# Attention steps on one core: norm products and value transposes placed between the logits and the weighted sums, strips taken two at a time

## The chip, the core and the metric

The kernel runs on one core of a Trainium2 chip. The core has a matrix engine (TensorE, written PE in the profile, with its weight loads as PEld), a vector engine (VectorE, DVE), a scalar engine (ScalarE, ACT), a general engine (GpSimd, POOL) and a queue engine (SyncE, SP) that here only issues DMA transfers. Each engine works through its own instructions in the order in which they were issued to it and waits on semaphores for the others. Matrix products land in PSUM, everything else in SBUF or device memory.

The metric is the device time of one execution in microseconds, as a median of runs.

## What is computed

The input is one image of 48 channels, 256 x 256. Two residual layers are applied, each to a group-normalised copy of its input. The first is the one that matters here:

```python
qkv = einsum('bchw,oc->bohw', gn(x), w_qkv)      # 48 -> 144 channels
qkv = dwconv3x3(qkv, w_dw)
q, k, v = split(qkv, 3)
# 4x4 patches; 8 heads; per head 96 numbers for each patch
q, k = q / |q|, k / |k|                          # norm over the 96
attn = softmax(q^T k * temperature, axis=-1)     # per head, over all patches
out  = v attn                                    # 'bhcn,bhnm->bhcm'
out  = einsum('bchw,oc->bohw', fold(out), w_proj)
x    = x + out
```

There are 4096 inner patches; the padding adds a border of patches whose values are zero and which only enter the softmax's sum. The second layer multiplies windows of 64 x 64 pixels by three small matrices (over width, height and channels); nothing of it is touched.

## The kernel before

**Stages.** First the input's statistics, the 1x1 convolution for heads 0 and 1, and the depthwise convolution of head 0. Then the attention, eight heads one after the other. Then the projection with the first residual (L718 to L780), and the second layer (L783 to L915). The attention is by far the longest stage, and only it is changed.

**Steps of the attention.** For each head h a loop runs over g = 0 to 15 (L637). One step takes two blocks of 128 queries:

- `scores` (L553) makes the logits of one block: 24 products of 128 x 128 by 128 x 512 in four PSUM tiles named big (L334); ScalarE takes the exponential of each tile into `e` and its row sums into `zs` (L562). A step makes the second block of its own pair and then the first block of the next step's pair, 48 products in a row.
- `normalised` (L571) makes, on VectorE, four small instructions for each block that end in `vn`, the block's values over its softmax sums (L581).
- `weigh` (L584) is called for k = 0 to 3. Each call runs 32 products with 64 columns of `e` as the stationary operand and `vn` as the moving one (L591), alternately on the lower and upper half of the array's columns; within a call the first two products use the first block's `vn`, the third and fourth the second block's, and so on. VectorE adds each call's tile to `oacc` (L602). TensorE shows two records for each of these float32 products, so a call is 64 records.

The tiles named big, for logits, weighted sums and strips alike, share three PSUM buffers in rotation: a tile can be written when the tile three places earlier has been read.

**Work for the next head, done in the same steps.** Rows of the next head's depthwise convolution pass through the steps as a pipeline: in step g row g starts (`n.first`, ScalarE), row g-1 (`d`) gets its taps (L228, three after the first logits and five after the second), its square (L239), its sums `reduce` (L243, after the weighted sum k = 0), its norm product `norm` (L247, one product of 126 x 126 by 126 x 64 on TensorE, two records) and the inverse root `root` (L251 to L268, twelve small VectorE instructions) after k = 2, and `scale` (L273) after k = 3. Row g-2 (`p`) is split into a high and a low part (L282 on ScalarE, L286 on GpSimd) and stored. So norm and root of a row run in steps g = 1 to 10 of heads 0 to 6.

**Other work in the steps.** `turn` (L542) transposes a tile of values with four small TensorE products into a PSUM tile named pst (L545) and copies it with ScalarE: one call after k = 0 in steps 1 to 6 of head 0, and two calls (after k = 0 and k = 2) in steps 11 to 14 of heads 0 to 6. `store` (L604) transposes finished results with four products (L608): two calls after k = 0 of step 0 for the head before, and two after each of k = 1, 2 and 3 in step 15. The PSUM tiles of norms, turns and stores share two buffers (tag "one"). In head 0 each of the 64 places (h, g, k) also runs one `Strip` (L162): two products of 48 x 108 by 48 x 512 (L177, four records), a ScalarE copy (L180), and its loads and stores on SP's queue. Three input tiles `xs` and three output tiles `ot` are shared by the strips in rotation.

**Order.** The attention is inside `tc.manual_schedule()` (L631), so the order of the calls in the loop is the order of the instructions on each engine and on each DMA queue:

```python
                    for k in range(NK):
                        s = (h * NG + g) * NK + k
                        weigh(h, g, blocks, k)
                        if k == 0 and d:
                            d.reduce()
```

Of the kernel before, what the change touches and what calls it, by code (L numbers as in the profile page):

```python
# [8 lines left out]
F32 = mybir.dt.float32  # L9
# [20 lines left out]
CR = 9  # L30
# [15 lines left out]
def conv_preact_kernel(  # L46
# [62 lines left out]
    for z in range(3):  # L109
        for j in range(CH):  # L110
            p = (z * CH + j) * 6
# [46 lines left out]
    def both_halves(t, y, n, base=0):  # L158

        return [t[:, base + s * HALF + y : base + s * HALF + y + n, :] for s in range(2)]  # L160

    class Strip:  # L162
# [24 lines left out]
        def store(self):  # L187
            for s, rows in enumerate(both_halves(t1[1], 2 * self.j, 2, base=1)):
                nc.sync.dma_start(out=rows, in_=self.ot[:, 2 * s : 2 * s + 2, :])
# [140 lines left out]
    def logits(ps, qt, kts, q0, j):  # L330

        for i in range(2):
            for r in range(3):
                nc.tensor.matmul(  # L334
                    ps[:, i, :],
                    lhsT=qt[:, r, q0 : q0 + 128],
                    rhs=kts[2 * j + i][:, r // 2, :],
                    start=(r == 0),
                    stop=(r == 2),
                )  # L340
# [58 lines left out]
    with tc.tile_pool(name="xn", bufs=1) as xnp, tc.tile_pool(name="cst", bufs=1) as cst, tc.tile_pool(  # L399
        name="nps", bufs=2, space=PSUM  # L400
# [23 lines left out]
        for g, (w, k) in enumerate(((wq, P2), (wr, C))):  # L424
            m = w.shape[1]
# [60 lines left out]
    with tc.If(nc.values_load(large) > 0):  # L486
        with tc.tile_pool(name="sps", bufs=2, space=PSUM) as sps:
            for j in range(HALF // 2):
                w = Strip(j)
# [5 lines left out]
        with tc.tile_pool(name="mk", bufs=NM) as mk, tc.tile_pool(name="mq", bufs=2) as mq, tc.tile_pool(  # L495
            name="mps", bufs=2, space=PSUM
# [23 lines left out]
    with tc.tile_pool(name="ahead", bufs=2) as ah, tc.tile_pool(name="ae", bufs=3) as ae, tc.tile_pool(  # L520
        name="asm", bufs=6
# [6 lines left out]
        def load_key(h, m, eng=nc.sync):  # L528
            keys[h, m] = ah.tile([128, 2, 512], F32R, name="kt", bufs=14)
            load_keys(keys[h, m], h, m, eng)  # L530

        def load_query(h, g):
            queries[h, g] = ah.tile([128, 3, 256], F32R, name="qt", bufs=2)
            load_queries(queries[h, g], h, g)

        def load_value(h, m):

            vt = ah.tile([HD, 4 * 128], F32, name="vt")
            load(vt, qkv[h][2, 2], m * 512, (m + 1) * 512)
            values[h, m] = vt  # L540

        def turn(h, m):  # L542
            ps = one.tile([128, 4, HD], F32, name="pst", tag="one")
            for i in range(4):
                nc.tensor.transpose(ps[:, i, :], values[h, m][:, i * 128 : (i + 1) * 128], ident[:HD, :HD])  # L545
            vT = ah.tile([128, 4, HD], F32, name="vT", bufs=9)
            nc.scalar.copy(vT, ps)
            values[h, m] = vT
# [4 lines left out]
        def scores(h, nb):  # L553

            b = h * NB + nb
            e = ae.tile([128, NT], F32, name="e")
            zs = asm.tile([128, 4], F32, name="zs")
            kts = [keys[h, m] for m in range(NM)]
            for j in range(4):
                ps = big.tile([128, 2, 512], F32, name="big")  # L560
                logits(ps, queries[h, nb // 2], kts, nb % 2 * 128, j)
                nc.scalar.activation(  # L562
                    e[:, j * 1024 : (j + 1) * 1024],
                    ps.rearrange("p a b -> p (a b)"),
                    AF.Exp,
                    bias=nmx[:, b : b + 1],
                    accum_out=zs[:, j : j + 1],
                )
            return h, nb, e, zs

        def normalised(h, nb, e, zs):  # L571

            b = h * NB + nb
            zt = asm.tile([128, 1], F32, name="zt")
            nc.vector.tensor_reduce(zt, zs, AX.X, ALU.add)  # L575
            zu = asm.tile([128, 1], F32, name="zu")
            nc.vector.scalar_tensor_tensor(zu, e0[:, b : b + 1], float(NBORDER), zt, ALU.mult, ALU.add)  # L577
            rz = asm.tile([128, 1], F32, name="rz")
            nc.vector.reciprocal(rz, zu)
            vn = asm.tile([128, HD], F32, name="vn")  # L580
            nc.vector.tensor_scalar_mul(vn, values[h, nb // 4][:, nb % 4, :], rz)  # L581
            return e, vn
# [44 lines left out]
        strips = [[Strip(s)] if s < HALF // 2 else [] for s in range(NH * NG * NK + 2)]  # L627
# [3 lines left out]
        with tc.manual_schedule():  # L631
            load_query(0, 1)
            block = scores(0, 0)
            for h in range(NH):
                more = h + 1 < NH
                rows = {r: Depthwise(h + 1, r) for r in range(CR + 1)} if more else {}
                for g in range(NG):  # L637
                    p, d, n = rows.get(g - 2), rows.get(g - 1), rows.get(g)

                    if h == 0 and 0 < g <= 6:  # L640
                        load_value(0, g + 1)
                    if more and CR + 2 <= g < CR + 6:
                        for m in range(2):
                            load_value(h + 1, (g - CR - 2) * 2 + m)
                    if more and CR + 3 <= g < CR + 6:
                        for m in range(2):
                            load_key(h + 1, (g - CR - 3) * 2 + m)

                    blocks = [normalised(*block)]
                    block = scores(h, g * G + 1)  # L650
                    if more and g == NG - 1:
                        load_key(h + 1, 6)
                        load_key(h + 1, 7, nc.gpsimd)
                    if g + 2 < NG:
                        load_query(h, g + 2)
                    elif more:
                        load_query(h + 1, g + 2 - NG)
                    if p:
                        p.store((2,))
                    if d:  # L660
                        for t in range(1, 4):
                            d.tap(t)
                    second = block
                    if g + 1 < NG:
                        block = scores(h, (g + 1) * G)
                    elif more:
                        block = scores(h + 1, 0)
                    blocks.append(normalised(*second))
                    if d:
                        for t in range(4, 9):  # L670
                            d.tap(t)

                    if g == 0 and rows:
                        rows[0].load()
                    if p:
                        p.high()
                    if d:
                        d.square()
                    if n:
                        n.first()  # L680
# [5 lines that stand above are left out]
                        if k == 0 and p:  # L686
                            p.low(nc.gpsimd)
                            p.store((0, 1))
                        for w in strips[s]:
                            w.run(big.tile([128, 2, 512], F32, name="big"))  # L690
                        for w in strips[s + 2]:
                            w.load()
                        for w in strips[s - 1] if s else []:
                            w.store()
                        if k == 2 and d:
                            d.norm()
                            d.root()
                        if k == 2 and g + 1 in rows:
                            rows[g + 1].load()
                        if k == 3 and d:  # L700
                            d.scale()
                        if h == 0 and 0 < g <= 6 and k == 0:
                            turn(0, g + 1)
                        if more and CR + 2 <= g < CR + 6 and k in (0, 2):
                            turn(h + 1, (g - CR - 2) * 2 + k // 2)

                        if g == 0 and h > 0 and k == 0:
                            for m in range(6, 8):
                                store(h - 1, m)
                        if g == NG - 1 and k > 0:  # L710
                            for m in range(2 * k - 2, 2 * k):
                                store(h, m)
            for m in range(6, 8):
                store(NH - 1, m)
# [6 lines left out]
    with tc.tile_pool(name="pj", bufs=3) as pj, tc.tile_pool(name="pjs", bufs=1) as pjs, tc.tile_pool(  # L721
        name="pps", bufs=3, space=PSUM
# [60 lines left out]
    with tc.tile_pool(name="lx", bufs=3) as lx, tc.tile_pool(name="lz", bufs=2) as lz, tc.tile_pool(  # L783
        name="lr", bufs=2
    ) as lr, tc.tile_pool(name="ly", bufs=4) as ly, tc.tile_pool(name="ps1", bufs=2, space=PSUM) as ps1, tc.tile_pool(
        name="ps2", bufs=2, space=PSUM
# [170 lines left out]
```

## Time and profile before

| what | value |
|---|---|
| median of three runs | 3743.46 us (3741.68 to 3744.67) |
| the profiled execution's own time | 3747.01 us |
| its span | 3745.2 us |
| TensorE busy in the span | 3515.0 us (94%) |
| VectorE busy | 2186.7 us (58%) |
| ScalarE busy | 1717.9 us (46%) |
| GpSimd busy | 548.3 us (15%) |
| logits, L334 | 1438.6 us in 6144 records |
| weighted sums, L591 | 1419.5 us in 32768 records |

The attention's first full step starts at 320.76 us and the last weighted sums end near 3265 us. A start time in the timeline is microseconds from the span's start. Where one engine works without a pause, the difference between the starts of two neighbouring groups is what the first of them costs, and this is the number that is used below; the busy time of a TensorE group has a modelled end and overlaps its successor by some hundredths of a microsecond.

### The profile page before, as it was taken

To read this page: it belongs to the slowest core of one execution; us is meant where nothing else is said; L and a number is where in the kernel's file an instruction comes from. 1 tells how busy PE (TensorE), PEld (TensorE's weight loads), DVE (VectorE), ACT (ScalarE), POOL (GpSimd) and SP (SyncE) were. 2 spreads that over 40 slices of the span, in tenths; PEclk is the share of its full clock that TensorE was granted. 3 is DMA by queue.
4 is the path that set the end of the run, shared out by engine and by line. 5 is a ranking of instruction groups with operands and counts; after the bars stand their busy time and mean duration, and the time that the engine had idled before them with its cause. 6 is when DMAs were issued, how large, how long until landed. Compare 5 with 4: busy or idle time off the path is not lost.

```text
span 3745.2 us, 100375 instructions
## 1 busy us (share of the span) xinstructions
PE 3515.0 (94%) x44252; PEld 2913.5 (78%) x44252; DVE 2186.7 (58%) x3514; ACT 1717.9 (46%) x2667; POOL 548.3 (15%) x628
## 2 busy tenths in 40 slices
PE   2869999999999999999999999999999999855998
PEld 1337777788888888888888888888888888713776
DVE  5454774189529943994499349925982222266564
ACT  0225665555545545554555455545554444300333
POOL 2040121012111211221122112201220000000011
PEclk9989999999999999999999999999999999966999
DMA  7465665433323332333233323332333100299784
GB/s 163 145 145 148 178 171 166 146 90 97 79 81 86 89 82 78 88 89 85 75 94 85 82 74 95 85 80 84 94 77 84 36 19 20 60 236 190 122 141 91
DMA packets 274147, 386.49 MB, mean 103 GB/s; under 512 B 77010, under 2 KB 211522, under 8 KB 269480
## 3 DMA queue, kind: packets, MB, share of 16 engines
q1 hardware_dynamic: 234790, 264.95, 27.2%
q0 software_dynamic: 35424, 106.40, 12.3%
q10 hardware_dynamic: 3490, 8.64, 1.1%
q8 instruction: 351, 5.75, 0.6%
q14 instruction: 92, 0.75, 0.1%
HBM read 234.76 MB, written 144.90 MB: 101 GB/s over the span
## 4 chain that ended last, share of the span: by engine, by line
PE 87%; DMA 4%; issue 1%; DVE 1%; SPq 0%; ACT 0%; POOL 0%; POOLq 0%; ACTq 0%; DVEq 0%
PE big L334 38%; PE big L591 37%; PE pb L855 4%; PE pa L833 2%; PE pc L872 2%; PE big L177 2%; DMA pxt<-in_x_dram 1%; PE pst L545 1%; PE pt L608 1%; DMA x1s<-pxt 1%; PE pn L247 1%; DMA pot<-os__70 1%; DMA kt<-qkv 0%; DVE pxt L745 0%; DMA lxq<-x1s 0%
## 5 line engine op out<-in xcount | busy, mean ns | idle before, releaser
L562 ACT ACTIVATE e<-big,nmx 128x1024 f32<-128x1024 f32 x1024 | 1144.3, 1118 | 825.7 <-PE big L334 624.2
L334 PE MATMUL big<-kt,qt 128*128 128x512 f32 x6144 | 1438.6, 393 | 28.3 <-DMA qt<-qkv 20.1
L591 PEld LDWEIGHTS big<-vn,e 128*64 128x64 f32 x32768 | 1361.8, 137 | 81.4 <-ACT e L562 45.1
L591 PE MATMUL big<-vn,e 128*64 128x96 f32 x32768 | 1419.5, 247 | 2.9 <-DVE vn L581 1.9
L334 PEld LDWEIGHTS big<-kt,qt 128*128 128x128 f32 x6144 | 1146.4, 188 | 290.0 <-issue 40.5
L602 DVE TENSOR_TENSOR oacc<-big,oacc 128x768 f32<-128x768 f32 x480 | 458.2, 955 | 703.7 <-PE big L591 703.7
L228 DVE SCALAR_TENSOR_TENSOR acc<-pad,dwt,acc 126x1024 f32<-126x1024 f32 x592 | 766.8, 1295 | 35.9 <-ACT acc L209 19.7
L286 POOL TENSOR_TENSOR ol<-o,oh 126x1024 fp32r<-126x1024 f32 x78 | 187.0, 2398 | 964.6 <-DVE ss L243 834.8
L575 DVE TENSOR_REDUCE zt<-zs 128x1 f32<-128x4 f32 x256 | 38.7, 151 | 342.3 <-ACT e L562 342.3
L562 ACT ACTIVATION_READ_ACCUMULATOR e<-big,nmx 128x1 f32 x1024 | 195.9, 191 | 0.0
L840 DVE TENSOR_TENSOR lzt<-pa,cbias 128x864 f32<-128x864 f32 (+1 forms) x88 | 137.0, 1628 | 100.0 <-PE pa L833 100.0
L862 ACT COPY lyt<-pb 128x512 f32<-128x512 f32 x144 | 84.5, 586 | 216.0 <-PE pb L855 216.0
L612 POOL DMA_DIRECT2D os__70<-oo x128 | 65.2, 515 | 598.9 <-ACT oo L610 598.8
L855 PEld LDWEIGHTS pb<-wsb,lzt 128*64 128x64 f32 x2304 | 126.2, 138 | 30.1 <-issue 21.9
L239 ACT ACTIVATE sq<-acc 126x1024 f32<-126x1024 f32 x74 | 78.3, 1058 | 152.1 <-issue 111.6
L273 DVE TENSOR_TENSOR o<-acc,y 126x1024 f32<-126x1024 f32 x74 | 147.6, 1994 | 0.0
L855 PE MATMUL pb<-wsb,lzt 128*64 128x128 f32 x2304 | 142.4, 279 | 3.3 <-issue 3.3
L738 PE MATMUL pps<-pot,wp 96*96 96x512 f32 x128 | 77.7, 775 | 69.9 <-DMA pot<-os__70 69.9
L292 POOL DMA_DIRECT2D qkv<-o x72 | 56.3, 781 | 528.0 <-DVE zu L577 483.3
L180 ACT ACTIVATE ot<-big,bias 108x1024 f32<-108x1024 f32 x64 | 71.1, 1113 | 131.0 <-PE big L177 73.2
L738 PEld LDWEIGHTS pps<-pot,wp 96*96 96x96 f32 x128 | 26.6, 216 | 120.6 <-issue 117.5
L209 ACT ACTIVATE acc<-pad,dwt 126x1024 f32<-126x1024 f32 x74 | 84.1, 1137 | 78.1 <-DMA pad<-t 78.1
(122 smaller groups left out, 1877.3 us busy)
## 6 DMA issues: line engine op xcount, KB each, us to landing
pad<-t SPq DMA_DIRECT2D x238, 254.0 KB
t<-ot SPq DMA_DIRECT2D x128, 217.7 KB
qkv<-ol POOLq DMA_DIRECT2D x78, 336.0 KB, 6.2
qkv<-oh POOLq DMA_DIRECT2D x70, 336.0 KB, 5.6
qt<-qkv SPq DMA_DIRECT2D x176, 96.0 KB
xs<-in_x_dram SPq DMA_DIRECT2D x128, 96.0 KB
os__70<-oo POOLq DMA_DIRECT2D x128, 96.0 KB, 2.1
pxt<-in_x_dram SPq DMA_DIRECT2D x16, 768.0 KB
```

The source lines that it names most:

```text
L209: nc.scalar.mul(self.acc, self.pad[:, 0:KS, 0:W], dwt[:, self.h, 0:1])
L228: nc.vector.scalar_tensor_tensor(self.acc, self.pad[:, dy : dy + KS, dx : dx + W], dwt[:, self.h, tap : tap + 1], self.acc, ALU.mult, ALU.add,
L273: nc.vector.tensor_tensor(self.o.rearrange("p (a b) x -> p a b x", a=KS), self.acc.rearrange("p a (x b) -> p a b x", b=KS), self.y.rearran ...
L286: eng.tensor_sub(self.ol, self.o, self.oh.bitcast(F32))
L334: nc.tensor.matmul(ps[:, i, :], lhsT=qt[:, r, q0 : q0 + 128], rhs=kts[2 * j + i][:, r // 2, :], start=(r == 0), stop=(r == 2),)
L562: nc.scalar.activation(e[:, j * 1024 : (j + 1) * 1024], ps.rearrange("p a b -> p (a b)"), AF.Exp, bias=nmx[:, b : b + 1], accum_out=zs[:, ...
L591: nc.tensor.matmul(ps[p : p + 64, j // 4, j % 4 * HD : (j % 4 + 1) * HD], lhsT=e[:, mb * 128 + p : mb * 128 + p + 64], rhs=vn, start=(i == 0),
L602: nc.vector.tensor_add(oaccs[h, k], ps[:, :, : 4 * HD], oaccs[h, k])
L738: nc.tensor.matmul(ps[:, i : i + 2, :], lhsT=wp, rhs=ot[:, ki * KS + i : ki * KS + i + 2, :], start=True, stop=True,)
L840: nc.vector.tensor_tensor(zv[:, :, y0 : y0 + n, :], pa[:, :, : n * T3 * C].rearrange("p s (y k) -> p s y k", y=n), cbias.rearrange("p (u v ...
L855: nc.tensor.matmul(pb[s * WS : (s + 1) * WS, i, :], lhsT=zts[u][:, t * C + c + i, :], rhs=wsb[:, t, :], start=True, stop=True,)
L862: nc.scalar.copy(yt[:, t, :], pb.rearrange("p i x -> p (i x)"))
```

## The change

Five calls change their places; no instruction is added, and none is removed.

- `norm` and `root` of a row move from after k = 2 of step g to the beginning of step g+1, in front of the logits, where the row is called `p`; `scale` moves from after k = 3 to the middle of the next step's logits.
- All `turn` calls of a step, and the two `store` calls of step 0, move in front of the first weighted sum, behind the logits.
- Strips run in pairs after k = 1 and k = 3. Their loads follow in pairs at the same places, and their stores follow in pairs at k = 2 and at k = 0 of the next step.

```diff
                     blocks = [normalised(*block)]
+                    if p:
+                        p.norm()
+                        p.root()
                     block = scores(h, g * G + 1)
...
                     if p:
+                        p.scale()
                         p.store((2,))
...
                     if g == 0 and rows:
                         rows[0].load()
+
+                    if h == 0 and 0 < g <= 6:
+                        turn(0, g + 1)
+                    if more and CR + 2 <= g < CR + 6:
+                        for m in range(2):
+                            turn(h + 1, (g - CR - 2) * 2 + m)
+                    if g == 0 and h > 0:
+                        for m in range(6, 8):
+                            store(h - 1, m)
                     if p:
                         p.high()
...
                             p.low(nc.gpsimd)
                             p.store((0, 1))
-                        for w in strips[s]:
-                            w.run(big.tile([128, 2, 512], F32, name="big"))
-                        for w in strips[s + 2]:
-                            w.load()
-                        for w in strips[s - 1] if s else []:
-                            w.store()
-                        if k == 2 and d:
-                            d.norm()
-                            d.root()
+                        if s % 2:
+                            for w in strips[s - 1] + strips[s]:
+                                w.run(big.tile([128, 2, 512], F32, name="big"))
+                            for w in strips[s + 1] + strips[s + 2]:
+                                w.load()
+                        elif s:
+                            for w in strips[s - 2] + strips[s - 1]:
+                                w.store()
                         if k == 2 and g + 1 in rows:
                             rows[g + 1].load()
-                        if k == 3 and d:
-                            d.scale()
-                        if h == 0 and 0 < g <= 6 and k == 0:
-                            turn(0, g + 1)
-                        if more and CR + 2 <= g < CR + 6 and k in (0, 2):
-                            turn(h + 1, (g - CR - 2) * 2 + k // 2)
-
-                        if g == 0 and h > 0 and k == 0:
-                            for m in range(6, 8):
-                                store(h - 1, m)
+
```

## The prediction

> **What bounds the kernel.** I read the page's busy times first, then the timeline of TensorE in single steps, then VectorE's timeline in the same steps. The page:
>
> ```profile
> PE 3515.0 (94%) x44252; PEld 2913.5 (78%) x44252; DVE 2186.7 (58%) x3514; ACT 1717.9 (46%) x2667; POOL 548.3 (15%) x628
> PE   2869999999999999999999999999999999855998
> PEclk9989999999999999999999999999999999966999
> ```
>
> In the fourth to the thirty-fourth slice TensorE is at nine tenths or more, from 320 us on without a pause, and its granted clock is 1.00 in every stretch of 200 us from 400 to 3000. So here the time of a step is the sum of what stands in TensorE's order, and whatever shortens that order shortens the kernel, as long as nobody makes TensorE wait. A step of head 4 with a norm product, and one of head 7, which has nothing between:
>
> ```profile
> 2264.02 8.14 PE L591 MATMUL big<-vn,e 128*64 128x96 f32 x192
> 2272.09 0.43 PE L247 MATMUL pn<-ss,same 126*126 126x64 f32 x2
> 2272.45 2.86 PE L591 MATMUL big<-vn,e 128*64 128x96 f32 x64
> 2275.24 11.17 PE L334 MATMUL big<-kt,qt 128*128 128x512 f32 x48
> ```
>
> ```profile
> 3110.00 11.17 PE L334 MATMUL big<-kt,qt 128*128 128x512 f32 x48
> 3121.10 10.78 PE L591 MATMUL big<-vn,e 128*64 128x96 f32 x256
> ```
>
> By start differences (the next logits start at 3131.81), 256 records of weighted sums cost 10.71 us, 192 cost 8.07, 64 cost 2.79: 2.64 for each 64, and **0.15 for each time the run is left**. The norm product costs 0.36 before a weighted sum. The whole step costs 22.33 against 21.81, so one tiny product costs 0.52.
>
> **What a small product costs elsewhere.** Transposes stand before weighted sums at 0.48 for four (472.12 to 472.60), but between logits:
>
> ```profile
> 291.56 0.49 PE L545 MATMUL pst<-ident,vt 96*128 96x96 f32 x4
> 291.83 1.18 PE L334 MATMUL big<-kt,qt 128*128 128x512 f32 x4
> 292.85 0.49 PE L545 MATMUL pst<-ident,vt 96*128 96x96 f32 x4
> 293.13 7.10 PE L334 MATMUL big<-kt,qt 128*128 128x512 f32 x30
> ```
>
> 0.28 (292.85 to 293.13): returning to weighted sums costs 0.20 that returning to logits does not. The result transposes (L608) say the same, 1.01 against 0.84. A norm product before logits isn't in the trace; 0.36 less 0.17 to 0.20 gives 0.16 to 0.19, and its bounds are 0.16 and the full 0.36. I take 0.18. Going from logits to transposes: logits records come every 0.227 us (11.17 for 48 less 5.73 for 24, over 24), so 48 take 10.88 and the change to weighted sums 0.22 of the 11.10. In the rows above four records take 1.02, that is 0.91 and 0.11. So I take 10.99 for logits before transposes, bounds 10.88 and 11.10, by that row.
>
> **TensorE, heads 1 to 6.** Steps as they are and as they become:
> - g=0 (two result transposes move ahead): 22.98 becomes 11.10+1.01+10.71 = 22.82, **-0.16** (also in head 7).
> - g=1 (its norm goes to g=2): 22.33 becomes 21.81, **-0.52**.
> - g=2 to 10: 0.18+11.10+10.71 = 21.99 instead of 22.33, **-0.34**, if nothing waits.
> - g=11 (a norm arrives, two turns join): 0.18+10.99+0.28+0.48+10.71 = 22.64 instead of 23.08, **-0.44**.
> - g=12 to 14: 10.99+0.28+0.48+10.71 = 22.46 instead of 23.10, **-0.64**.
> - g=15 is unchanged.
>
> **VectorE is the new risk.** The root and scale now stand between the step's start and the second block's vn, which the third product of the first weighted sum needs. Its order in a step, from before:
>
> ```profile
> 2254.67 2.00 DVE L273 TENSOR_TENSOR o<-acc,y 126x1024 f32<-126x1024 f32 x1
> 2256.57 0.16 DVE L575 TENSOR_REDUCE zt<-zs 128x1 f32<-128x4 f32 x1
> ...
> 2257.35 3.93 DVE L228 SCALAR_TENSOR_TENSOR acc<-pad,dwt,acc 126x1024 f32<-126x1024 f32 x3
> 2261.19 0.15 DVE L575 TENSOR_REDUCE zt<-zs 128x1 f32<-128x4 f32 x1
> ...
> 2261.77 0.27 DVE L581 TENSOR_SCALAR vn<-vT,rz 128x96 f32<-128x96 f32 x1
> 2261.95 6.57 DVE L228 SCALAR_TENSOR_TENSOR acc<-pad,dwt,acc 126x1024 f32<-126x1024 f32 x5
> 2268.44 0.95 DVE L602 TENSOR_TENSOR oacc<-big,oacc 128x768 f32<-128x768 f32 x1
> 2269.69 1.22 DVE L243 TENSOR_REDUCE ss<-sq 126x64 f32<-126x1024 f32 x1 [0.31 <-ACT sq L239]
> ```
>
> Today vn is ready at 2262.04, 2 us before the weighted sum at 2264.02. After the change, counted from the norm product's start: the last addition starts at 0.12 (as after every run of weighted sums) and takes 0.87, the first block's four instructions 0.78, the root 3.05 (2250.75 to 2253.80), the scale 1.90, three taps 3.84, the second block's four until vn 0.58, vn 0.27: 11.41. TensorE sees it 0.05 later:
>
> ```profile
> 3246.54 0.39 PE L591 MATMUL big<-vn,e 128*64 128x96 f32 x4
> 3248.79 5.34 PE L591 MATMUL big<-vn,e 128*64 128x96 f32 x124 [1.87 <-DVE vn L581]
> ```
>
> Here vn started at 3248.47 and ended at 3248.74; four records, two products, had run, and nothing but the wait is lost. So vn counts from 11.46; TensorE reaches its fifth record at 0.18+11.10+0.165 = 11.45. They meet: a wait of 0.01, period 22.00, -0.33. Further on: five taps until 17.81, the first addition, the reduce at 19.06 (ScalarE's square, as now, 1.25 after the taps), the second addition until 21.07. The fourth weighted sum needs the first addition's buffer at 19.4 and has it by 18.8. VectorE is free at 22.0, and its next addition is due at 22.12: it fits with 0.1 to spare. That thin margin is the main risk. A norm that costs 0.36 would not add to a wait; it replaces it.
>
> Sum for a head: 0.16+0.52+9x0.33+0.44+3x0.64 = 6.0; six heads **-36.1**, head 7 -0.16.
>
> **Head 0, with strips.** A pair costs 2x1.045; two runs of 128 records 5.43 each (1014.35 to 1019.78); together 15.04 instead of 4x(2.79+1.045) = 15.34. But three buffers go round: the third weighted sum takes that of the second, which the second addition frees, and that stands behind the reduce. VectorE, now starting with the root at 0.47: 3.05+1.90+3.84+0.76+6.48 makes 16.50, reduce at 17.71, second addition from 18.85, free at 19.87. TensorE wants it at 0.18+11.10+5.43+2.09 = 18.80, or 19.16 with a turn. So a new wait of 1.08 or 0.71, and a step of 27.39 either way. g=2 to 6: 27.28 becomes 27.39, +0.55 in all; g=7 to 10: from 26.80, +2.36; g=1: 27.30 to 26.51; g=11: 27.39 to 26.97; g=12 to 14: 27.42 to 26.79; g=15 loses one interruption, 0.16; g=0 waits for ScalarE's first row either way. Sum **-0.4**. On SP's queue the stores of a pair come one call later, behind the query loads, and the loads of a pair's second input wait for the pair's first product; each still lands some 8 us ahead of its use. The value loads, issued 0 to 5 us into the step, now are needed at 11.2 instead of 15 us; 168 KB landed in 3.5 us elsewhere.
>
> **Sum.** -36.7 on the profiled execution's 3747.0 gives 3710.3. Its own time lies 3.5 above the median of the runs, so the median becomes 3706.8, **3707 us**.
>
> **A rule that speaks against it.** GpSimd's subtraction (2.36 us) runs from the reduce's end, at 20.3, until 0.6 of the next step; in before it never ran beside a VectorE instruction with two inputs in SBUF, and after the change it still ends before the root. The Trainium skill, "SBUF — State Buffer", section "SBUF: two separate sides", says that such an instruction and a GpSimd one exclude each other for the whole instruction. By it the sum stands as long as they don't meet, and a VectorE chain 1.6 us later would lose up to the subtraction's rest; no run here shows that. On the other side "TensorEngine Tiling (Array Packing)", "Key Properties", says that changing the tiling mode drains TensorE; logits and transposes have one mode, and by it the 0.11 above would be gone too, some 3 us more gained.
>
> **Rivals.**
> - *The interruptions cost the same in the new place*: 0.36 for a norm, 0.48 for every turn, 11.10 for logits. Then g=2 to 10 gain 0.16 each, g=12 to 14 0.33, g=11 loses 0.05: 3.9 a head, 23.5 for six, head 0 loses some 2: 3722 us. The 0.28 and 0.84 speak against it. 13%.
> - *Head 0's waits are longer* (a pair's copies, stores or the value loads come late): 1 to 3 us in each of 16 steps, 16 to 48 us: 3723 to 3755 us. For it: TensorE did wait 2.6 us for a strip's copy at 315.88. Against: the leads above. 10%.
> - *vn comes later than worked out*, by 0.3 us in 54 steps: 16 us, 3723 us. 10%.
> - *Slower: VectorE's chain becomes the bound.* Place: root and scale ahead of the second vn. Every 0.1 us costs 5.4; from 0.7 us the gain is gone, from 0.82 the kernel is slower by 0.2%. The price is bounded by a whole subtraction falling into the chain, 54x2.36 = 127 us, 3834 us. The margins above speak against it. 5%.
> - The forecast, 3697 to 3718 us: 62%. Its lower end is head 0 without its waits (8 us) and a strip pair 0.1 cheaper (3 us).
>
> Some 0.2% (7.5 us) is what a measurement can tell from no change. The range, **3697 to 3736**, takes in the forecast, the first and third rivals and part of the second. Faster (below 3736): 62+13+10+4 = 89, with a little taken off for what I overlooked 87%; within 0.2%: 6%; slower: 7%.
>
> **What will show it.** Right: steps g=2 to 10 of heads 1 to 6 at 22.0, the norm product before logits at 0.18, g=12 to 14 at 22.46, VectorE almost without a pause in g=2 to 10; head 0 at 27.39 for g=2 to 10 with a wait for an addition (L602) before the third weighted sum. Wrong: TensorE waiting for vn (L581) by more than 0.1 at the first weighted sum, strips waiting for `ot` or `xs`, transposes waiting for `vt`.

## The result and the profile after

The changed kernel takes 3737.34 us (median of 20 runs, 3731.5 to 3748.8), the kernel before 3741.89 in 20 runs beside it: a ratio of 0.999 [0.9982, 0.9999]. The change gains some 4.5 us where 37 were forecast; by the interval it is between 0.4 and 6.7. The profiled execution took 3738.23 us, its span is 3736.4.

The page of the changed kernel, with its line of the chain that ended last (shares of the span by engine):

```profile
PE 3478.8 (93%) x44252; PEld 2909.0 (78%) x44252; DVE 2218.8 (59%) x3514; ACT 1706.6 (46%) x2667; POOL 544.7 (15%) x628
...
PE   2869999999999999999999999999999999955998
...
PEclk9989999999999999999999999999999999966999
...
PE 65%; DVE 16%; issue 5%; DMA 4%; ACT 1%; SPq 1%; POOL 0%; DVEq 0%; ACTq 0%; POOLq 0%
```

The same line of the chain in the kernel before:

```profile
PE 87%; DMA 4%; issue 1%; DVE 1%; SPq 0%; ACT 0%; POOL 0%; POOLq 0%; ACTq 0%; DVEq 0%
```

TensorE is busy for 36 us less than before, and the span shrinks by only 9. So TensorE's own work became shorter, and it now waits. That 36 lies so close to the forecast gain is partly chance: the forecast had new waits of head 0 in its sum, and the busy time counts a part of each wait as work. The chain says for whom TensorE waits: VectorE has 16% of it, and had 1% before. The slices can't show this, since a wait of 0.4 us in 22 leaves a nine a nine. VectorE executes the same 3514 instructions and is busy for 32 us longer: some of them must have become slower. Among the groups, one moved by far more than the rest: L260, the integer step that starts the inverse root, takes 576 ns on average instead of 195, and with 70 executions that alone is 26.6 of the 32 us.

TensorE's timeline in head 4 (start, duration, then the wait in front of it and who ended it):

```profile
2270.13 0.43 PE L247 MATMUL pn<-ss,same 126*126 126x64 f32 x2
2270.37 11.16 PE L334 MATMUL big<-kt,qt 128*128 128x512 f32 x48
2281.46 0.39 PE L591 MATMUL big<-vn,e 128*64 128x96 f32 x4
2282.26 10.62 PE L591 MATMUL big<-vn,e 128*64 128x96 f32 x252 [0.41 <-DVE vn L581]
2292.80 0.43 PE L247 MATMUL pn<-ss,same 126*126 126x64 f32 x2
```

The norm product before the logits costs 0.24 (2270.13 to 2270.37). The logits take 11.09, four records run, and then TensorE stands until 2282.26: 0.80 from 2281.46, of which four records explain 0.165. The rest, 0.63, is the wait; the profile shows 0.41 of it as idle. From norm to norm the step is 22.67 us, not 22.00, and more than the 22.33 of before. VectorE in the same step:

```profile
2271.89 0.22 DVE L251 TENSOR_SCALAR n<-pn 126x64 f32<-126x64 f32 x1
2272.14 0.69 DVE L260 TENSOR_SCALAR y<-n 126x64 int32<-126x64 int32 x1
...
2275.20 0.31 DVE L268 TENSOR_SCALAR y<-y,nmul,nadd 126x64 f32<-126x64 f32 x1
2275.60 2.00 DVE L273 TENSOR_TENSOR o<-acc,y 126x1024 f32<-126x1024 f32 x1
2277.53 3.91 DVE L228 SCALAR_TENSOR_TENSOR acc<-pad,dwt,acc 126x1024 f32<-126x1024 f32 x3
...
2281.93 0.27 DVE L581 TENSOR_SCALAR vn<-vT,rz 128x96 f32<-128x96 f32 x1
```

vn ends at 2282.20, 12.07 after the norm product's start, and the fifth record starts at 12.13. The working had 11.46. The 0.67 lies in two places. L260 takes 0.69 instead of 0.20, that is 0.50; and the scale L273 starts 0.40 after L268's start, where the last addition, which stood there before, started 0.22 after it, that is 0.18. What GpSimd did meanwhile in the changed kernel:

```profile
2268.49 2.37 POOL L286 TENSOR_TENSOR ol<-o,oh 126x1024 fp32r<-126x1024 f32 x1 [12.52 <-DVE ss L243]
2270.81 0.98 POOL L292 DMA_DIRECT2D qkv<-oh  x1
2271.75 1.06 POOL L292 DMA_DIRECT2D qkv<-ol  x1
```

The subtraction L286 ends at 2270.86, well ahead of the root, as the prediction said. But behind it GpSimd issues the transfers of the two parts, each for about 1 us, and L260 stands from 0.39 us into the second one until its very end (2272.81 against 2272.83). In the kernel before the same instructions lay like this, first GpSimd, then VectorE:

```profile
2250.99 1.00 POOL L292 DMA_DIRECT2D qkv<-oh  x1
2252.00 1.00 POOL L292 DMA_DIRECT2D qkv<-ol  x1
```

```profile
2251.00 0.20 DVE L260 TENSOR_SCALAR y<-n 126x64 int32<-126x64 int32 x1
```

There L260 began within 0.04 us of the beginning of an issue, in all 54 steps, and ran through in 0.20. Behind it come nine instructions (L265 to L267) that ran through the issues in 0.22 to 0.23, and L268 begins at 2253.58, when both issues are over. In the changed kernel it begins 0.29 to 0.41 into the second issue in all 54 and takes 0.68 to 0.72. The trace of before never had it in that place.

One row inside the changed kernel supports the reading. In g=2 of heads 1 to 6 there is a norm, but no parts to be sent yet; L260 takes 0.20 there, and the step takes 22.19.

All steps, from logits to logits (a step holds the norm product of the next one). Each number is the usual one of its row; single steps differ, such as g=0 of head 1, which takes 23.15 in the changed kernel:

| steps | before | after | kernel "best" below |
|---|---|---|---|
| heads 1 to 6: g=0 | 22.98 | 22.69 | 22.70 |
| g=1 | 22.33 | 22.08 | 22.08 |
| g=2 | 22.33 | 22.19 | 22.03 |
| g=3 to 10 | 22.33 | 22.67 | 22.03 |
| g=11 | 23.08 | 22.47 | 22.46 |
| g=12 to 14 | 23.10 | 22.51 | 22.51 |
| g=15 | 24.99 | 25.01 | 25.01 |
| head 0: g=2 to 10 | 27.28, from g=7 26.80 | 27.38 | 26.33, from g=7 26.08 |

The attention, from the logits of g=1 in head 0 to those of g=1 in head 7, went from 2614.7 to 2612.3 us: -2.4. The rest of the profiled difference lies ahead of and behind the attention, where no instruction was changed, and is how two executions differ.

In head 0 a pair of strips stands behind 128 records. TensorE in the changed kernel:

```profile
447.41 5.50 PE L591 MATMUL big<-vn,e 128*64 128x96 f32 x128 [0.99 <-DVE oacc L602]
452.84 1.97 PE L177 MATMUL big<-xs,wr 48*108 48x512 f32 x8
454.74 0.43 PE L247 MATMUL pn<-ss,same 126*126 126x64 f32 x2
```

That is the foretold wait for the second addition, in the foretold place. By start differences it is 1.03 to 1.06 in g=2 to 6, where a transpose stands ahead of it, and 1.37 to 1.41 in g=7 to 10; 0.71 and 1.08 were forecast.

### The profile page after: what moved, and what is told of

The parts are those of the page before. It is cut to its first block, busy times and chain, and to the rows that moved or that the text cites. A ratio compares the mean times of both kernels' runs of the same rounds, so it can differ in the third digit from the quotient of the medians.

```text
span 3736.4 us, 100361 instructions
## 1 busy us (share of the span) xinstructions
PE 3478.8 (93%) x44252; PEld 2909.0 (78%) x44252; DVE 2218.8 (59%) x3514; ACT 1706.6 (46%) x2667; POOL 544.7 (15%) x628
## 4 chain that ended last, share of the span: by engine, by line
PE 65%; DVE 16%; issue 5%; DMA 4%; ACT 1%; SPq 1%; POOL 0%; DVEq 0%; ACTq 0%; POOLq 0%
PE big L591 35%; PE big L334 21%; DVE acc L228 7%; PE pb L858 4%; PE pa L836 2%; PE pc L875 2%; DVE oacc L602 1%; DMA x1s<-pxt 1%; PE big L177 1%; DMA pxt<-in_x_dram 1%; DVE y L267 1%; DVE z L265 1%; DVE z L266 1%; DVE y L260 1%; DVE vn L581 1%
## 5 line engine op out<-in xcount | busy, mean ns | idle before, releaser
L591 PE MATMUL big<-vn,e 128*64 128x96 f32 x32768 | 1400.5, 247 | 32.4 <-DVE vn L581 21.3
L602 DVE TENSOR_TENSOR oacc<-big,oacc 128x768 f32<-128x768 f32 x480 | 453.5, 954 | 677.3 <-PE big L591 671.1
L286 POOL TENSOR_TENSOR ol<-o,oh 126x1024 fp32r<-126x1024 f32 x78 | 187.4, 2403 | 897.4 <-DVE ss L243 786.4
L273 DVE TENSOR_TENSOR o<-acc,y 126x1024 f32<-126x1024 f32 x74 | 148.4, 2005 | 6.3
```

What stands on the lines that cost most here:

```text
L273: nc.vector.tensor_tensor(self.o.rearrange("p (a b) x -> p a b x", a=KS), self.acc.rearrange("p a (x b) -> p a b x", b=KS), self.y.rearran ...
L286: eng.tensor_sub(self.ol, self.o, self.oh.bitcast(F32))
L591: nc.tensor.matmul(ps[p : p + 64, j // 4, j % 4 * HD : (j % 4 + 1) * HD], lhsT=e[:, mb * 128 + p : mb * 128 + p + 64], rhs=vn, start=(i == 0),
L602: nc.vector.tensor_add(oaccs[h, k], ps[:, :, : 4 * HD], oaccs[h, k])
```

## Experiments

Two theories stood against each other. **A**: L260 is held up by the transfer issues of GpSimd, and with the late scale it delays the second vn; the rest of the change is worth what was forecast. **B**: VectorE's chain in its new order is too long by itself, whatever GpSimd does. The ratios are to the kernel before, on the same chip.

### One part alone

The norm product, the root and the scale moved, nothing else ("norm_only", against before):

```diff
                     blocks = [normalised(*block)]
+                    if p:
+                        p.norm()
+                        p.root()
...
                     if p:
+                        p.scale()
...
-                        if k == 2 and d:
-                            d.norm()
-                            d.root()
...
-                        if k == 3 and d:
-                            d.scale()
```

> Only the norm product, root and scale are moved as in the change; turns, stores and strips stay as in before. Theory A (VectorE's chain to the second vn is 0.67 us longer than I worked out: 0.5 because the root's second instruction, L260, stands still while GpSimd issues the transfer of the low part, 0.18 because the scale now follows the root's last instruction directly): in heads 1 to 6 the steps g=3 to 10 take 22.67 us against 22.33, g=2 some 22.2, so this part alone loses about 2.3 us a head, ratio to before about 1.003 (some 3753 us). Rival B (the chain is not the cause, the gain was lost elsewhere): the steps take 22.0 and the ratio is about 0.995.

Measured: 3760.73 us, ratio 1.005 [1.0038, 1.0063]. This part alone is a loss, larger than expected. Its steps g=3 to 10 take 22.67, as in the whole change. VectorE in g=2, where GpSimd issues nothing, and in g=3; then GpSimd in g=3:

```profile
2250.16 0.20 DVE L260 TENSOR_SCALAR y<-n 126x64 int32<-126x64 int32 x1
...
2272.35 0.72 DVE L260 TENSOR_SCALAR y<-n 126x64 int32<-126x64 int32 x1
```

```profile
2272.04 1.01 POOL L292 DMA_DIRECT2D qkv<-ol  x1
```

2272.35 is 0.31 into the issue, and 2273.07 is its end within 0.02. In head 0 this kernel also waits for a strip's copy, which the expectation had not counted, and most steps there take 27.86 instead of 27.28; TensorE there:

```profile
454.57 2.86 PE L591 MATMUL big<-vn,e 128*64 128x96 f32 x64 [0.64 <-ACT ot L180]
```

The transposes moved alone ("turns_only", against before):

```diff
+                    if h == 0 and 0 < g <= 6:
+                        turn(0, g + 1)
+                    if more and CR + 2 <= g < CR + 6:
+                        for m in range(2):
+                            turn(h + 1, (g - CR - 2) * 2 + m)
+                    if g == 0 and h > 0:
+                        for m in range(6, 8):
+                            store(h - 1, m)
...
-                        if h == 0 and 0 < g <= 6 and k == 0:
-                            turn(0, g + 1)
-                        if more and CR + 2 <= g < CR + 6 and k in (0, 2):
-                            turn(h + 1, (g - CR - 2) * 2 + k // 2)
-                        if g == 0 and h > 0 and k == 0:
-                            for m in range(6, 8):
-                                store(h - 1, m)
```

> Only the turns of all steps and the two stores of step 0 are moved in front of the first weighted sum. Theory A: nothing waits, the steps g=11 to 14 of heads 1 to 6 take 22.5 instead of 23.1, some 2.4 us a head, with the stores and head 0 some 18 us in all, ratio about 0.995. Rival B (moved turns give nothing once other things are equal): ratio 1.000.

Measured: 3727.37 us, 0.996 [0.9945, 0.9974]. The steps g=11 to 14 take 22.48 to 22.53, as forecast. Some is given back in head 0, where the value loads now come late (TensorE's timeline):

```profile
474.99 0.55 PE L545 MATMUL pst<-ident,vt 96*128 96x96 f32 x4 [1.31 <-DMA vt<-qkv]
```

With the strips in pairs, in the whole change, the same transposes don't wait.

The strips in pairs alone ("strips_only", against before):

```diff
-                        for w in strips[s]:
-                            w.run(big.tile([128, 2, 512], F32, name="big"))
-                        for w in strips[s + 2]:
-                            w.load()
-                        for w in strips[s - 1] if s else []:
-                            w.store()
+                        if s % 2:
+                            for w in strips[s - 1] + strips[s]:
+                                w.run(big.tile([128, 2, 512], F32, name="big"))
+                            for w in strips[s + 1] + strips[s + 2]:
+                                w.load()
+                        elif s:
+                            for w in strips[s - 2] + strips[s - 1]:
+                                w.store()
```

> Only the strips are paired. Theory A: a pair costs 1.90 instead of 2.09 us, and without the moved root the second addition is in time, so there is no wait for L602 before the third weighted sum: head 0 gains some 8 us, ratio about 0.998. Rival B (the wait in head 0 comes from pairing alone): the third weighted sum waits some 1 us in each of nine steps and the gain is near 0.

Measured: 3742.01 us, 1.0009 [0.9997, 1.0021]: no gain that the interval tells from none, where A had expected a small one. Most steps of head 0 take 26.3 to 27.0 us, so the pairs do save there, and no step waits for the second addition: that wait, which B had foretold, takes the moved root as well. But the profiled execution loses it again in one place. TensorE, and then two stretches of the same execution (length, then for each engine its busy time and instructions, PEclk, DMA share, GB/s):

```profile
434.16 3.87 PE L177 MATMUL big<-xs,wr 48*108 48x512 f32 x8 [5.19 <-DMA xs<-in_x_dram]
437.96 12.85 PE L334 MATMUL big<-kt,qt 128*128 128x512 f32 x48
```

```profile
434.00:438.00 4.00, 3.84 (x9) 1.53 (x9) 3.50 (x3) 1.11 (x1) 0.00 (x0) 0.50 0.89 203
442.00:446.00 4.00, 4.00 (x19) 3.31 (x18) 0.00 (x0) 3.13 (x7) 0.00 (x0) 1.00 0.52 163
```

A strip's input came late, TensorE stood for 5.19 us, and then the granted clock was 0.50: eight records took 3.87 instead of 1.97, and the logits 12.85 instead of 11.17. With 5.19, 1.90 and 1.68 the wait costs 8.8 us in all. On SP's queue the four loads of the pair were issued from 425.00 to 432.08, behind twelve query loads (414.20 to 421.38) and four stores (421.48 to 424.96). Whether every execution of this kernel has the wait, one profile can't say.

### The transfer issues taken away from GpSimd

The whole change, with the two stores of heads 1 to 6 on SP's queue ("after_sp", against after):

```diff
                             p.low(nc.gpsimd)
-                            p.store((0, 1))
+                            p.store((0, 1), nc.sync if h else nc.gpsimd)
```

> The whole change, and in heads 1 to 6 the stores of the high and low parts are issued from SP's queue instead of GpSimd's. Theory A: L260 takes 0.20 instead of 0.70 us, the second vn comes 0.5 earlier, steps g=3 to 10 take 22.2 instead of 22.67, some 23 us gained on the changed kernel, ratio to before about 0.993. Rival B (L260 is slow for another reason, or the chain is long all the same): L260 stays at 0.7 or the steps stay at 22.67, ratio 0.999.

Measured: 3711.42 us, 0.992 [0.9902, 0.9937]. TensorE, and L260, in the same step of head 4:

```profile
2258.14 0.43 PE L247 MATMUL pn<-ss,same 126*126 126x64 f32 x2
2258.38 11.15 PE L334 MATMUL big<-kt,qt 128*128 128x512 f32 x48
2269.46 10.96 PE L591 MATMUL big<-vn,e 128*64 128x96 f32 x256
2280.34 0.43 PE L247 MATMUL pn<-ss,same 126*126 126x64 f32 x2
```

```profile
2260.14 0.20 DVE L260 TENSOR_SCALAR y<-n 126x64 int32<-126x64 int32 x1
```

L260 takes 0.20 again, and the step 22.20 instead of 22.67. VectorE's order is the same as in the changed kernel, so B falls as the main cause. Weighted sums of 10.88 (2269.46 to 2280.34) instead of 10.71 show what remains, the 0.17 by which vn still comes late.

### The chain shortened, and the reduce moved

One tap fewer between the scale and the second vn ("after_taps"), and this together with the stores on SP ("after_sp_taps"); against after:

```diff
-                        for t in range(1, 4):
+                        for t in range(1, 3):
...
-                        for t in range(4, 9):
+                        for t in range(3, 9):
```

> The changed kernel with two taps instead of three ahead of the second vn (six behind it). The vn is then ready some 1.3 us earlier and TensorE has nothing to wait for there. Theory A (the block on L260 makes VectorE's whole round longer than TensorE's): VectorE has only 0.19 us of pause in a round of 22.67, so the steps g=3 to 10 come down to 22.48 only, some 9 us gained on the changed kernel, ratio to before about 0.9965. Rival B (only the place of the vn in VectorE's order counts): the steps come down to TensorE's own 22.04, some 30 us, ratio about 0.991.

> The changed kernel with both: the high and low parts of heads 1 to 6 stored from SP's queue, and two taps ahead of the second vn. Theory A: L260 at 0.20 and the vn in time, VectorE's round is 21.98 and TensorE's 22.04, so the steps g=2 to 10 take 22.05 against 22.19 with the queue alone, some 8 us less than that, ratio about 0.990. Rival B: no further gain once the queue is moved, ratio 0.992.

Measured: 3705.38 us, 0.9903 [0.9887, 0.9919], and 3704.37 us, 0.9901 [0.9883, 0.992]; both have steps of 22.03. That the taps add something to the moved queue is seen in the steps (22.20 in after_sp); the intervals of the times overlap. For after_taps that is B's number and not A's. But the profile shows why the run doesn't decide between them: GpSimd and VectorE of after_taps,

```profile
2255.63 1.06 POOL L292 DMA_DIRECT2D qkv<-ol  x1
```

```profile
2255.87 0.20 DVE L260 TENSOR_SCALAR y<-n 126x64 int32<-126x64 int32 x1
```

L260 now begins 0.24 into the issue (0.13 to 0.26 in all 54 steps), and runs through. A shift of some 0.15 us had taken it out of the place where it is held. The edit had removed the suspected cause as well as the length.

The reduce after k = 1 instead of k = 0, so that the second addition no longer stands behind it ("after_reduce", against after), and all three together ("after_all"):

```diff
-                        if k == 0 and d:
+                        if k == 1 and d:
                             d.reduce()
```

> The changed kernel with the reduce behind the second addition instead of the first. Theory A: in head 0 the third weighted sum no longer waits for the second addition, nine steps come down from 27.38 to 26.4 or below, some 9 us; in heads 1 to 6 GpSimd's work starts 0.9 us later, the issue of the high part instead of the low part now falls on L260, which stays slow, and the steps stay near 22.6: ratio about 0.9965. Rival B (L260 is slow only beside the second of the two issues): it falls to 0.2 and the steps to some 22.2, ratio about 0.990.

> The changed kernel with all three: stores of heads 1 to 6 from SP's queue, two taps ahead of the second vn, the reduce behind the second addition. Theory A: steps g=2 to 10 of heads 1 to 6 at 22.04, head 0 some 9 us shorter, ratio to before about 0.9875 (some 3694 us), faster than both kernels. Rival B (one of the three only shifts the wait elsewhere): no better than 0.992.

Measured: 3718.19 us, 0.9934 [0.9915, 0.9954], and 3701.56 us, 0.9885 [0.9868, 0.9903]. In both, head 0's wait is gone (steps of 26.33 and 26.08). In heads 1 to 6 after_reduce takes 22.41, which is neither number expected of it. Its GpSimd and VectorE:

```profile
2259.32 0.99 POOL L292 DMA_DIRECT2D qkv<-oh  x1
```

```profile
2259.74 0.60 DVE L581 TENSOR_SCALAR vn<-vT,rz 128x96 f32<-128x96 f32 x1
2259.92 0.42 DVE L251 TENSOR_SCALAR n<-pn 126x64 f32<-126x64 f32 x1
2260.40 0.20 DVE L260 TENSOR_SCALAR y<-n 126x64 int32<-126x64 int32 x1
```

GpSimd's work begins later here, and another instruction falls 0.42 into an issue: the first block's vn, L581, which takes 0.60 instead of 0.27 and ends with the issue. So it isn't something about L260. And in after_all, without these issues, it is the subtraction that meets VectorE, GpSimd first:

```profile
2266.17 2.37 POOL L286 TENSOR_TENSOR ol<-o,oh 126x1024 fp32r<-126x1024 f32 x1 [13.04 <-issue]
```

```profile
2268.11 0.46 DVE L577 SCALAR_TENSOR_TENSOR zu<-e,zt 128x1 f32<-128x1 f32 x1
```

L577, with two inputs in SBUF, takes 0.46 instead of 0.16 and ends with the subtraction (2268.57 against 2268.54). Its steps are 22.03, in part up to 22.15.

### The block put back by a shift

To tell A from B after all, one more small VectorE instruction, whose result nobody reads, ahead of L251: in after_taps ("taps_nudge"), and in after_sp_taps ("sp_nudge"). B charges both for the instruction; A lets only the first one lose, because there L260 is pushed back into the held place.

```diff
+            for _ in range(0 if on_scalar else 1):
+                nc.vector.tensor_scalar_max(self.pool.tile([NP1, PX], F32, name="jk", bufs=1), self.pn, 1e-24)
```

> The kernel with two taps ahead of the second vn, and one more small VectorE instruction (a copy of L251 into a tile nobody reads, 0.25 us from start to start) ahead of the root, so that L260 starts some 0.5 us instead of 0.24 after the issue of the low part begins. Theory A (an L260 that starts later than 0.28 us into such an issue stands until its end; that run missed it by 0.04): L260 goes from 0.20 to 0.75 us, VectorE's round from 21.98 to 22.7 and with it the steps g=3 to 10 from 22.03 to some 22.7, ratio to before about 1.000. Rival B (only the vn's place in VectorE's order counts): L260 stays at 0.20 and the steps at 22.03 to 22.25, where the latter is the added instruction alone, ratio 0.990 to 0.993.

> The same added instruction in the kernel with two taps ahead of the second vn and the stores of heads 1 to 6 on SP's queue, so that GpSimd issues nothing beside the root. Theory A: L260 stays at 0.20, and the steps go from 22.03 to 22.23 only, by the added instruction in VectorE's round; ratio to before about 0.993, some 25 us less than the kernel before in this list. Rival B: no difference between the two kernels with the added instruction.

Measured: 3734.5 us, 0.9963 [0.9948, 0.9978], and 3704.06 us, 0.9897 [0.988, 0.9913]. The lines are two higher here, so L260 is L262. GpSimd and VectorE of taps_nudge:

```profile
2270.36 1.05 POOL L294 DMA_DIRECT2D qkv<-ol  x1
```

```profile
2270.29 0.22 DVE L252 TENSOR_SCALAR jk<-pn 126x64 f32<-126x64 f32 x1
2270.42 0.21 DVE L253 TENSOR_SCALAR n<-pn 126x64 f32<-126x64 f32 x1
2270.67 0.77 DVE L262 TENSOR_SCALAR y<-n 126x64 int32<-126x64 int32 x1
```

and the same instruction in sp_nudge:

```profile
2258.52 0.19 DVE L262 TENSOR_SCALAR y<-n 126x64 int32<-126x64 int32 x1
```

The added instruction moves L251 by 0.13 us (2270.29 to 2270.42). L260 now begins 0.31 into the issue instead of 0.24, and it takes 0.77. One step earlier in the same head, g=3, it begins 0.21 into the issue, which starts at 2248.34, and runs through:

```profile
2248.55 0.19 DVE L262 TENSOR_SCALAR y<-n 126x64 int32<-126x64 int32 x1
```

That step takes 22.03, as g=3 does in every head, and g=4 to 10 take 22.59 to 22.70. The two kernels differ by nothing but the queue of two stores, and by 30 us. In sp_nudge the same steps take 22.03 to 22.11, so the added instruction itself costs at most 0.08, less than the 0.20 that A had counted for it, and by its time sp_nudge can't be told from after_sp_taps. A holds in the durations and in the order of the kernels; its ratio for taps_nudge, 1.000, was too high. In taps_nudge the wait shows in another place, though; TensorE:

```profile
2288.20 2.86 PE L593 MATMUL big<-vn,e 128*64 128x96 f32 x64 [0.36 <-DVE oacc L604]
```

The second vn is in time, one tap being gone from ahead of it, but VectorE has no pause left in the step except the 0.31 us for ScalarE's square, so the 0.57 by which L260 is longer comes out at its next deadline, the addition (here L604) whose buffer the fourth weighted sum needs. This part of B is right: VectorE is nearly full, and whatever lengthens it lengthens the step.

### The version that beats both

All three edits, with the reduce moved in head 0 alone, where its wait was ("best", label after_best; against after, beside the edits of taps and stores shown above):

```diff
-                        if k == 0 and d:
+                        if k == (0 if h else 1) and d:
                             d.reduce()
```

> The changed kernel with the stores of heads 1 to 6 on SP's queue, two taps ahead of the second vn, and the reduce behind the second addition in head 0 alone. Theory A: head 0's steps at 26.1 to 26.3 and the steps g=2 to 10 of heads 1 to 6 at 22.03 in all of them, where the reduce moved in every head let GpSimd's subtraction fall on the next step's L577 and left 22.14; some 3 us better than that kernel, ratio to before about 0.988. Rival B: the reduce's place makes no difference in heads 1 to 6, same time as with it moved everywhere.

Measured: 3692.88 us, 0.9869 [0.9851, 0.9887]. Its chain by engines, and TensorE in head 4:

```profile
PE 87%; DMA 4%; issue 1%; DVE 1%; ACT 0%; SPq 0%; POOL 0%; POOLq 0%; ACTq 0%
```

```profile
2261.03 0.43 PE L247 MATMUL pn<-ss,same 126*126 126x64 f32 x2
2261.28 11.15 PE L334 MATMUL big<-kt,qt 128*128 128x512 f32 x48
2272.36 10.78 PE L591 MATMUL big<-vn,e 128*64 128x96 f32 x256
2283.07 0.43 PE L247 MATMUL pn<-ss,same 126*126 126x64 f32 x2
```

0.25 + 11.08 + 10.71 = 22.04: the step is the sum of TensorE's own work, without a wait, and VectorE is out of the chain again. The same stretch of the attention takes 2568.3 us, 46.4 less than before. Against after_all the intervals of the times overlap; that the reduce's place matters in heads 1 to 6 is seen in the steps, which are 22.03 in all of g=2 to 10, and in the stretch of the attention (2568.3 against 2571.7).

## Why the prediction was wrong

**What held.** TensorE's prices, nearly all. Two transposes of values in front of the weighted sums cost 0.75 (0.76 forecast), one 0.42 (0.48), logits before them 10.98 to 11.06 (10.99), result transposes 0.97 (1.01). A norm product before logits costs 0.24, between the 0.18 taken and the bound of 0.36. The steps g=11 and g=12 to 14 came out at 22.47 and 22.51 (22.64 less its 0.18, and 22.46). TensorE's own work is 46.4 us shorter: this is what "best" saves, which has the same order on TensorE and hardly a wait. The forecast's 36.7 and the 8 us of waits that it had put into head 0 make 45.

**What came out by luck.** Head 0's step, 27.38 against a forecast of 27.39. A pair of strips costs 1.90 instead of 2.09. The first pair's saving is lost in the wait behind it; the second pair's isn't, and it should have made the step 0.19 shorter. But the second addition came 0.19 late (19.04 after the norm product's start instead of 18.85), since the scale stands directly behind L268 in head 0 too. The two errors cancel.

**What failed is the root's term of 3.05 in the chain to the second vn.** From L251's start to the scale's start it measured 3.71 (2271.89 to 2275.60). 0.50 of it is L260, 0.18 the scale directly behind L268. The issue is thus the larger part of the error, and the later scale a second one, which no issue explains: it stays in after_sp. vn came at 12.13 instead of 11.46, TensorE reached its fifth record at 0.24+11.09+0.165 = 11.50, and the wait is 0.63 instead of 0.01. In steps g=3 to 10 of six heads that is 48 x 0.67 = 32.2 us, nearly all of the 34.3 by which the attention missed its forecast. Of the rest, which is small and of both signs, g=2 is 1.1 (6 x 0.19), g=12 to 14 0.9, one longer step in head 6 1.1, and head 0 did better by 1.7.

**The root's duration was carried over from a place where something else protected it.** In before, L260 began together with a transfer issue and slipped through. The prediction did set GpSimd's subtraction against the moved root, and rightly said that it ends first; it did not set the two issues behind the subtraction against it, although the timeline of GpSimd showed them, 2 us long, where the root would land. Their remainder, up to 1 us each, should have been a bound of that term.

**The rivals.** "VectorE's chain becomes the bound" and "vn comes later" named the right place, and 0.67 us lies close to the 0.7 at which the gain was to be gone. Together they had 15%. Against them stood "the margins above", which were 0.01 us for vn and 0.1 for VectorE as a whole, while the bounds of the terms in the same sum were wider than that. That the interruptions might cost the same in their new place is refuted for the transposes by turns_only and for the norm product by its 0.24. The price of this rival was also added up wrongly: its own terms (0.16 + 0.52 + 9x0.16 - 0.05 + 3x0.33) make 3.1 us a head and not 3.9, some 3727 us and not 3722.

**The parts.** Alone, the norm part costs 0.5%, the transposes gain 0.4%, and the strips show no gain. With the two stores moved to another queue the same change is worth 0.8%, and with the chain shortened by a tap as well 1.0%.

## What to carry to other kernels

Before a duration is carried to a new place, lay every other engine's rows beside that place, transfer issues among them: a row holds only beside the neighbours it was measured with. A margin smaller than the uncertainty of the terms that make it counts as none, and in a ring of two engines whatever exceeds it comes out in full in every step. And an edit that shortens a chain also shifts it; where a cause depends on the position, take the suspected neighbour away rather than the length.

## What the runs showed of the hardware that was not expected

- A VectorE instruction TENSOR_SCALAR with its input in SBUF that begins 0.28 us or more into a GpSimd transfer issue of some 1.0 us stands until the issue ends; one that begins at 0.26 or earlier runs through. L260: 0.20 at 0.01 to 0.26, 0.67 to 0.79 at 0.28 to 0.41; L581: some 0.6 at 0.41 to 0.44, and only 0.27 to 0.37 at 0.66 and later, when little of the issue is left. The TENSOR_TENSOR and SCALAR_TENSOR_TENSOR instructions of the root (L265 to L267), with two inputs, ran through such issues in 0.22 to 0.23. The limit isn't the same everywhere: L581, 0.27 long, ran through at 0.20 into issues of 0.79 us and took 0.53 at 0.24 into one of 0.73 (sp_nudge). Whether it counts from the instruction's start or from its end, and why it lies there, no run shows.
- The Trainium skill, "SBUF — State Buffer", section "SBUF: two separate sides", says that VectorE and GpSimd share a pair of ports that one of them holds for a whole instruction: against any GpSimd work if VectorE runs in a two-port performance mode, and against GpSimd work that reads SBUF if the VectorE instruction has two inputs there. Both halves fit what was seen: the TENSOR_SCALARs are held by issues and the two-input ones aren't, and L577 is held by the subtraction (0.46 instead of 0.16). The subtraction can hold L260 too: in strips_only it took 0.37 once, at 1322.21, until the subtraction's end, while L251, whose input is in PSUM, ran beside it in 0.21 to 0.22. The first 0.26 us, in which an issue holds nobody up, the page doesn't state. Which mode the TENSOR_SCALARs ran in, no run shows.
- After a pause of 5.19 us TensorE came back at a granted clock of 0.50 and had 1.00 again some 8 us later; after pauses of 0.99 us it stayed at 1.00. This one long wait cost 8.8 us, 1.7 times its length.
- The scale (L273), which needs the result of L268 just ahead of it on VectorE, began 0.40 us after that one's start, 0.09 after its end; the last addition (L602), which doesn't need it, began after 0.22, ahead of its end. No fixed price follows from this: inside the root, where each instruction needs the one before, they follow each other at 0.23 to 0.26, some 0.03 after the end.
